# Layer 2's projections: 192 channels contracted as 128 + 64 rows instead of 96 + 96

## The chip, the cores and the metric

The kernel runs on one core of one Trainium2 chip. The metric is the device time of one execution in microseconds (us); what is quoted is the median over runs. Everything in the kernel is fp32. The engines of the core work side by side: TensorE (PE; its weight loads are listed apart as PEld), VectorE (DVE), ScalarE (ACT), GpSimd (POOL), and SyncE (SP), which here issues nearly all DMAs. A DMA is carried out by some or all of 16 DMA engines.

## The reference

Four layers are applied to an image batch x of shape (4, 64, 64, 192), each as `x = x + layer(groupnorm(x))`. Layers 0, 1 and 3 are selective scans (state-space models) over rows and columns. The change touches only layer 2, a gated Toeplitz mixer with D1 = 576 inner channels:

```python
p = silu(x @ p_w.T + p_b)            # x: normalized input, 192 channels -> 576
q = silu(x @ q_w.T + q_b)
v = silu(x @ v_w.T + v_b)
# a1, a2: 128 Toeplitz coefficients per channel, from a small MLP and a decay
qv = q * v
o1 = toeplitz(qv along w, a1)
o2 = toeplitz(qv along h, a2)
out = (p * (o1 + o2)) @ o_w.T + o_b
```

The three projections p, q and v contract 192 channels. They are the matmuls that the change rearranges; `o_w` contracts 576 channels and stays as it is.

## The kernel before, in words

Names: B = 4 images, L = 4096 pixels each, C = 192 channels kept in DRAM as KC = 2 halves of PC = 96 (partition, half, pixel), chunks of T = 512 pixels, NCH = 8 chunks per image, D1 = 576 inner channels as KD = 6 tiles of PD = 96. All of layer 2 is in `toeplitz`, and it runs after layer 1's scans and before layer 3's. It has three parts.

**Normalization.** Per image, layer 1's parts are added to the input, the sum goes to DRAM as `t_x` and its group norm as `t_xn`.

**The q/v part** (pool `t_*`). For each inner tile t (6) the two Toeplitz matrices `mat` are loaded (four DMAs, L931); for each group g of two images (2), so in twelve passes, it does:

- 16 chunks. Each loads `xn`, 96 x 2 x 512 (L60, the helper `load`), computes q and v (L944: two matmuls each, one for every half of the channels, accumulated in one PSUM tile each), applies Silu on ACT (L948) and multiplies into `qv` on DVE (L951).
- two calls of `toeplitz_way`: PE transposes (L1006), 64x64 matmuls with the matrices (L1014), transposes back (L1019), with evacuations on DVE and ACT.
- two stores of the result to DRAM, `t_o` (L956).

The pool `t_s` has two buffers per name, so the load of chunk i+2 can be issued only when PE has finished reading chunk i. The PSUM pool has four one-bank buffers under one tag.

**The p part** (pool `p_*`), for 32 chunks: load `xn`, `xr` (the residual) and `o` (`t_o`); six tiles of p (L975, two matmuls each), Silu (L978), multiply by `o` on DVE (L979), project back with `o_w` (L984: 2 x 6 matmuls), add the residual on DVE (L987), store (L990).

An fp32 matmul appears in the trace as two LDWEIGHTS/MATMUL pairs, called passes here; so a 192-channel product of one 96-channel tile over 512 pixels is 2 matmuls and 4 passes.

Instructions are written in program order and put into each engine's queue by the Tile framework, which may move independent work ahead; an engine then runs its queue in order. SP runs its queue in order too: a DMA that waits for a buffer holds back the DMAs behind it.

Two other places are used for comparison. `fetch` (L312) loads a scan operand twice, once into each half of the partitions, with one DMA:

```python
one = pools[name].tile([128, T], F32, name=name)
src = job["deltas" if name == "both" else "dtus"][key * 64 : (key + 1) * 64, :]
nc.sync.dma_start(one, src.unsqueeze(0).broadcast_to([2, 64, T]))
```

`step_size` (L253) multiplies 12 rows at partitions 32 to 43 and 12 rows at 96 to 107, into two PSUM tiles of 128 channels and 256 pixels.

Of the kernel before, what the change touches and what calls it, by code (L numbers as in the profile page):

```python
# [7 lines left out]
F32 = mybir.dt.float32  # L8
AF = mybir.ActivationFunctionType
# [4 lines left out]
B, HW, L = 4, 64, 4096  # L14
C = 192
PC, KC = 96, 2
# [3 lines left out]
T = 512  # L20
# [16 lines left out]
class Kernel:  # L37
# [807 lines left out]
    def toeplitz(self, x_in, parts, x_out):  # L845

        tc, nc, ins = self.tc, self.nc, self.i
        pre = "L2_"
        xn_d, x_d = self.image_tiles("t_xn"), self.image_tiles("t_x")
        o_d = [self.dram.tile([PD, KD, L], F32, name=f"t_o{b}") for b in range(B)]  # L850
        coef = [self.dram.tile([D1, 128], F32, name=f"t_a{j}") for j in range(2)]
        M = 127
        with (
            tc.tile_pool(name="n", bufs=2) as pn,
            tc.tile_pool(name="n_w", bufs=1) as pw,
            tc.tile_pool(name="n_ps", bufs=2, space=PSUM) as psum,
        ):
            fb = self.load(pw, "fb", ins["L1_fc_b"])
            for b in range(B):
                x = pn.tile([PC, KC, L], F32, name="x")  # L860
                rows, cols = (pn.tile([PC, KC, L], F32, name="part") for _ in range(2))
                for k in range(KC):
                    for to, of in ((x, x_in[b]), (rows, parts[b][0]), (cols, parts[b][1])):
                        nc.sync.dma_start(to[:, k, :], of[:, k, :])
                for k in range(KC):
                    nc.vector.scalar_tensor_tensor(
                        x[:, k, :], x[:, k, :], fb[:, k : k + 1], rows[:, k, :], ALU.add, ALU.add
                    )
                    by_row = x[:, k, :].rearrange("p (a b) -> p a b", b=HW)
                    nc.vector.tensor_add(by_row, by_row, cols[:, k, :].rearrange("p (b a) -> p a b", b=HW))  # L870
                    nc.sync.dma_start(x_d[b][:, k, :], x[:, k, :])
                self.group_norm(x, pn, psum)
                nc.sync.dma_start(xn_d[b], x)

            pos = self.load(pw, "pos", ins["c_pos"])
            power = pw.tile([PD, 128], F32, name="power")
            nc.sync.dma_start(power, ins["c_power"].broadcast_to([PD, 128]))
            rate = self.load(pw, "rate", ins[f"{pre}slope"])
            nc.vector.tensor_scalar(rate, rate, 0.0, 1.0, ALU.max, ALU.min)
            nc.vector.tensor_scalar(rate, rate, 1.0 - 0.95, 0.95, ALU.mult, ALU.add)  # L880
            nc.scalar.activation(rate, rate, AF.Ln)
            decay = pw.tile([PD, KD, 128], F32, name="decay")
            for t in range(KD):
                nc.scalar.activation(decay[:, t, :], power, AF.Exp, scale=rate[:, t : t + 1])
            for j in range(2):
                q = f"{pre}t{j + 1}_"
                w0 = self.load(pw, "w0", ins[q + "w0"])
                b0 = self.load(pw, "b0", ins[q + "b0"])
                ws = self.load(pw, "ws", ins[q + "ws"])
                bs = self.load(pw, "bs", ins[q + "bs"])  # L890
                wo = self.load(pw, "wo", ins[q + "wo"])
                bo = self.load(pw, "bo", ins[q + "bo"])
                ps = psum.tile([32, 128], F32, name="mlp_ps")
                nc.tensor.matmul(ps, w0, pos, start=True, stop=True)
                h = pn.tile([32, 128], F32, name="mlp_h")
                nc.scalar.activation(h, ps, AF.Relu, bias=b0)
                for i in range(3):
                    ps = psum.tile([32, 128], F32, name="mlp_ps")
                    nc.tensor.matmul(ps, ws[:, i, :], h, start=True, stop=True)
                    h = pn.tile([32, 128], F32, name="mlp_h")  # L900
                    nc.scalar.activation(h, ps, AF.Relu, bias=bs[:, i : i + 1])
                for t in range(KD):
                    ps = psum.tile([PD, 128], F32, name="a_ps")
                    nc.tensor.matmul(ps, wo[:, t * PD : (t + 1) * PD], h, start=True, stop=True)
                    a = pn.tile([PD, 128], F32, name="a")
                    nc.vector.scalar_tensor_tensor(
                        a, ps, bo[:, t : t + 1], decay[:, t, :], ALU.add, ALU.mult
                    )
                    nc.sync.dma_start(coef[j][t * PD : (t + 1) * PD, :], a)
# [4 lines left out]
        with (  # L914
            tc.tile_pool(name="t_w", bufs=1) as pw,
            tc.tile_pool(name="t_big", bufs=1) as big,
            tc.tile_pool(name="t_s", bufs=2) as sp,
            tc.tile_pool(name="t_ps", bufs=4, space=PSUM) as psum,
        ):
            wq, wv = (self.load(pw, n, ins[f"{pre}{n}"]) for n in ("q_w", "v_w"))  # L920
            bq, bv = (self.load(pw, n, ins[f"{pre}{n}"]) for n in ("q_b", "v_b"))
            for t in range(KD):
                ch = slice(t * PD, (t + 1) * PD)

                mats = []
                for j in range(2):
                    m = big.tile([128, PD, HW], F32, name=f"mat{j}")
                    a = coef[j][ch, :]
                    src = bass.AP(a.tensor, a.offset, [[1, HW], [128, PD], [1, HW]])
                    for half in range(2):  # L930
                        nc.sync.dma_start(m[half * HW : (half + 1) * HW], src)  # L931
                    mats.append(m)
                for g in range(B // G):

                    qv = big.tile([PD, G, L], F32, name="qv")
                    for b in range(G):
                        for c in range(NCH):
                            s = slice(c * T, (c + 1) * T)
                            xn = self.load(sp, "xn", xn_d[g * G + b][:, :, s])
                            two = []  # L940
                            for wt, bias, name in ((wq, bq, "q"), (wv, bv, "v")):
                                ps = psum.tile([PD, T], F32, name=f"{name}_ps", tag="ps")
                                for k in range(KC):
                                    nc.tensor.matmul(  # L944
                                        ps, wt[:, k, ch], xn[:, k, :], start=k == 0, stop=k == KC - 1
                                    )
                                r = sp.tile([PD, T], F32, name=name)
                                nc.scalar.activation(r, ps, AF.Silu, bias=bias[:, t : t + 1])  # L948
                                two.append(r)
                            turned = qv[:, b, L - (c + 1) * T : L - c * T][:, ::-1]  # L950
                            nc.vector.tensor_mul(turned, two[0], two[1])  # L951
                    o = big.tile([PD, G, L], F32, name="o")
                    for j in range(2):
                        self.toeplitz_way(j, qv, o, mats[j], big, psum, NI)
                    for b in range(G):
                        nc.sync.dma_start(o_d[g * G + b][:, t, :], o[:, b, :])  # L956

        with (
# [1 line left out]
            tc.tile_pool(name="p_s", bufs=2) as sp,  # L960
            tc.tile_pool(name="p_ps", bufs=4, space=PSUM) as psum,
        ):
            wp, bp = self.load(pw, "wp", ins[f"{pre}p_w"]), self.load(pw, "bp", ins[f"{pre}p_b"])
            wo, bo = self.load(pw, "wo", ins[f"{pre}o_w"]), self.load(pw, "bo", ins[f"{pre}o_b"])
            for b in range(B):
                for c in range(NCH):
                    s = slice(c * T, (c + 1) * T)
                    xn = self.load(sp, "xn", xn_d[b][:, :, s])
                    xr = self.load(sp, "xr", x_d[b][:, :, s])
                    o = self.load(sp, "o", o_d[b][:, :, s])  # L970
                    p = sp.tile([PD, KD, T], F32, name="p")
                    for t in range(KD):
                        ps = psum.tile([PD, T], F32, name="p_ps")
                        for k in range(KC):
                            nc.tensor.matmul(  # L975
                                ps, wp[:, k, t * PD : (t + 1) * PD], xn[:, k, :], start=k == 0, stop=k == KC - 1
                            )
                        nc.scalar.activation(p[:, t, :], ps, AF.Silu, bias=bp[:, t : t + 1])  # L978
                    nc.vector.tensor_mul(p, p, o)  # L979
                    xo = sp.tile([PC, KC, T], F32, name="xo")  # L980
                    for m in range(KC):
# [6 lines left out]
                            xo[:, m, :], ps, bo[:, m : m + 1], xr[:, m, :], ALU.add, ALU.add  # L988
                        )
                    nc.sync.dma_start(x_out[b][:, :, s], xo)  # L990

    def toeplitz_way(self, j, qv, o, mat, big, psum, NI):

# [159 lines left out]
```

## Time and profile before

| | us |
|---|---|
| median of 3 runs | 31505.68 (31467.85 to 31518.7) |
| the profiled execution | 31496.9 |
| its span | 31495.0 |
| busy: PE | 28016.1 (89%) |
| busy: PEld | 13777.8 (44%) |
| busy: DVE | 22496.5 (71%) |
| busy: ACT | 23230.4 (74%) |
| busy: POOL | 22921.2 (73%) |

The span is the time from the first to the last instruction of one profiled execution. A group line gives the source line, engine, operation, tiles (output <- inputs), shapes and count, then busy time and mean duration of one, then the idle time just before them with what ended it. A MATMUL's duration includes the pipeline's latency; what counts for throughput is the distance between starts.

Layer 2 lies between about 22,030 us and 25,110 us of the span, 3.1 ms of 31.5. The rest of the span belongs to the scans of layers 0, 1 and 3.

### The profile page before, as it was taken

The numbers are of one execution on the slowest core, as the hardware profiler recorded it, in microseconds if no ns is written. First come the engines' busy times: TensorE is split into PE (matmuls) and PEld (weight loads), VectorE is DVE, ScalarE is ACT, GpSimd is POOL, SyncE is SP. The second block draws the span as 40 slices with busy tenths as digits, with TensorE's granted clock in tenths as the row PEclk, the third lists the DMA queues.
The fourth block names the chain that finished last, engine by engine and source line by source line (L and its number), as shares of the span: only waits on it lengthen the run. The fifth ranks groups of instructions, "written<-read, shape, count | busy, mean of one in ns | idle before, by whom it ended". The sixth has DMA issues, their size and how long they took to land.

```text
span 31495.0 us, 452842 instructions
## 1 busy us (share of the span) xinstructions
PE 28016.1 (89%) x164120; PEld 13777.8 (44%) x164120; DVE 22496.5 (71%) x16587; ACT 23230.4 (74%) x50559; POOL 22921.2 (73%) x9863
## 2 busy tenths in 40 slices
PE   8998998998899699999999999999588988888888
PEld 4554554554455344444444444444355343434344
DVE  7887887888788677777777777777433267677767
ACT  7885885887688488888888888888123187878788
POOL 7885885887688488888888888888000086867777
PEclk9999998999999899999999999999789999999999
DMA  3333333334333433233332333333533454444444
GB/s 105 101 100 114 103 99 115 100 98 112 102 102 100 134 94 93 93 98 98 98 99 92 94 94 96 98 99 98 133 73 71 109 133 121 129 126 127 124 127 125
DMA packets 1586996, 3327.52 MB, mean 106 GB/s; under 512 B 354981, under 2 KB 374166, under 8 KB 1569142
## 3 DMA queue, kind: packets, MB, share of 16 engines
q1 hardware_dynamic: 1418870, 3021.63, 35.1%
q10 hardware_dynamic: 165888, 276.91, 2.6%
q8 instruction: 1299, 21.28, 0.3%
q14 instruction: 939, 7.69, 0.1%
HBM read 2138.38 MB, written 656.08 MB: 89 GB/s over the span
## 4 chain that ended last, share of the span: by engine, by line
PE 39%; DVE 14%; POOL 14%; ACT 13%; DMA 10%; issue 7%; SPq 2%; ACTq 0%; DVEq 0%; POOLq 0%
PE b L360 16%; POOL hc L405 11%; DVE h L400 8%; PE y L423 8%; ACT diag L318 5%; ACT dA L383 4%; DVE h L393 3%; DMA xn<-m_col 3%; DMA xn<-m_row 2%; PE in_ps L777 2%; POOL bs L337 2%; SPq L325 2%; PE yt_ps L1014 2%; PE conv_ps L509 2%; DMA xn<-t_xn 2%
## 5 line engine op out<-in xcount | busy, mean ns | idle before, releaser
L405 POOL TENSOR_TENSOR hc<-h,c 128x1024 f32<-128x1024 f32 x7680 | 18176.9, 2384 | 3019.2 <-DVE h L393 1288.0
L360 PE MATMUL b<-diag,dtuT 128*64 128x256 f32 x98304 | 12662.5, 392 | 955.3 <-DVE h L400 829.9
L360 PEld LDWEIGHTS b<-diag,dtuT 128*64 128x64 f32 x98304 | 7451.4, 140 | 6835.4 <-issue 3023.8
L400 DVE TENSOR_TENSOR_SCAN h<-dA,carry,b 128x512 f32<-128x512 f32 x6720 | 8187.4, 1264 | 1696.7 <-PE b L360 875.4
L423 PE MATMUL y<-hc,fold 128*64 128x512 f32 x30720 | 8832.2, 601 | 579.8 <-POOL hc L405 566.2
L383 ACT ACTIVATE dA<-both,A 128x512 f32<-128x512 f32 (+1 forms) x12288 | 8306.5, 711 | 305.7 <-DVE h L393 181.0
L393 DVE TENSOR_TENSOR_SCAN h<-dA,b 128x1024 f32<-128x1024 f32 x2304 | 5251.9, 2284 | 2064.3 <-PE b L360 900.9
L318 ACT ACTIVATE diag<-ident,bt 128x128 f32<-128x128 f32 x20480 | 6514.8, 391 | 123.5 <-ACT b L383 83.2
L337 POOL TENSOR_TENSOR bs<-dtu,bc 128x1024 f32<-128x1024 f32 x1536 | 3639.0, 2369 | 300.0 <-DMA dtu<-dtu 172.2
L423 PEld LDWEIGHTS y<-hc,fold 128*64 128x64 f32 x30720 | 2462.3, 138 | 2969.2 <-POOL hc L405 1263.2
L477 POOL MEMSET pad<- 128x13068 f32 (+1 forms) x8 | 73.5, 9187 | 3972.7 <-DMA cw<-in_L_conv_w 3005.2
L383 ACT ACTIVATE b<-both,A 128x504 f32<-128x504 f32 (+1 forms) x3072 | 2077.4, 676 | 283.0 <-DVE h L400 237.0
L393 DVE TENSOR_TENSOR_SCAN h<-b,bs 128x1024 f32<-128x1024 f32 x768 | 1754.3, 2284 | 658.6 <-ACT b L383 387.6
L403 ACT COPY carry<-h 128x2 f32<-128x2 f32 x4608 | 849.6, 184 | 1233.8 <-DVE h L400 1015.3
L400 DVE TENSOR_TENSOR_SCAN h<-b,carry,bs 128x512 f32<-128x512 f32 x1344 | 1638.2, 1259 | 105.5 <-POOL hc L405 94.2
L400 DVE TENSOR_TENSOR_SCAN h<-dA,b 128x512 f32<-128x512 f32 x960 | 1112.4, 1205 | 425.3 <-ACT dA L383 165.4
L383 ACT ACT_TABLE_LOAD x1018 | 1306.1, 1283 | 16.8 <-ACT b L371 0.3
L777 PE MATMUL in_ps<-xn,in_w 96*128 96x512 f32 x1536 | 943.6, 746 | 333.4 <-DMA xn<-m_row 173.3
L794 DVE SCALAR_TENSOR_TENSOR u<-in_ps,conv_w,u 128x504 f32<-128x504 f32 (+2 forms) x1152 | 835.8, 725 | 475.3 <-ACT u L789 454.0
L269 DVE TENSOR_TENSOR dtu<-delta,u 128x1536 f32<-128x1536 f32 (+1 forms) x256 | 607.4, 2373 | 541.6 <-ACT delta L268 541.6
L278 PEld LDWEIGHTS dtu_ps<-ident,dtu 128*128 128x128 f32 (+1 forms) x4096 | 421.5, 142 | 874.2 <-issue 554.0
L777 PE MATMUL z_ps<-xn,in_w 96*128 96x512 f32 x1536 | 761.7, 618 | 0.3 <-ACT dtuT L281 0.2
(163 smaller groups left out, 21940.7 us busy)
## 6 DMA issues: line engine op xcount, KB each, us to landing
c<-bc_dram SPq DMA_DIRECT2D x3072, 256.0 KB
both<-delta SPq DMA_DIRECT2D x2048, 128.0 KB
bc<-bc_dram SPq DMA_DIRECT2D x768, 256.0 KB
both<-delta_dram SPq DMA_DIRECT2D x768, 256.0 KB
dtu<-dtu_dram SPq DMA_DIRECT2D x768, 256.0 KB
dtu<-dtu SPq DMA_DIRECT2D x1280, 128.0 KB
L_y<-out ACTq DMA_DIRECT2D x512, 256.0 KB
u<-L_u SPq DMA_DIRECT2D x160, 768.0 KB
```

Of the source, the lines that this page charges most:

```text
L318: nc.scalar.activation(to, self.ident, AF.Copy, scale=of)
L325: nc.sync.dma_start(one[q * 64 : (q + 1) * 64, :], src.unsqueeze(0).broadcast_to([64, 2 * T]))
L337: self.nc.gpsimd.tensor_mul(by(b), dtu, by(job["bbc"][p]))
L360: nc.tensor.matmul(to, job["dtuT"][:, k, g * 64 : (g + 1) * 64], job["diag"][p][:, k, 2 * q : 2 * q + 2, :], start=True, stop=True,)
L383: nc.scalar.activation(to[n], of, AF.Exp, scale=w["A"][:, g, 2 * p + n : 2 * p + n + 1])
L393: nc.vector.tensor_tensor_scan(h[:, way], dA[:, way], b[:, way], 0.0, ALU.mult, ALU.add)
L400: nc.vector.tensor_tensor_scan(hn[:, n, way], dA[:, n, way], by_n[:, n, way], start, ALU.mult, ALU.add)
L403: nc.scalar.copy(carry[g, p], hn[:, :, 0 if rev else T - 1])
L405: nc.gpsimd.tensor_mul(hc, h, job["cbc"][p])
L423: nc.tensor.matmul(y[c * 64 : (c + 1) * 64, :], self.fold, of, start=first == 0 and n == 0, stop=last == LAST and n == 1)
L777: nc.tensor.matmul(ps, w["in_w"][:, k, to + t * P : to + (t + 1) * P], job["xn"][:, k, :], start=k == 0, stop=k == KC - 1,)
L794: nc.vector.scalar_tensor_tensor(u[:, :, to], ps[:, :, of], tap(3 - j), u[:, :, to], ALU.mult, ALU.add)
```

## The change

`t_xn` is stored in DRAM as 192 plain rows. The weights of q, v and p are cut into a piece of the first 128 channels and a piece of the last 64; the second piece is held twice, in partitions 0 to 63 and in 64 to 127 (`load_apart`). The pixels of a chunk come as two tiles of 128 partitions: the first 128 channels, and the last 64 twice (`load_pixels`, two DMAs). Two results at a time are computed (`project_two`): q and v of a chunk, or two neighbouring tiles of p. Each gets one matmul over 128 rows; then each gets one over 64 rows, the first result from partitions 0 to 63 and the second from 64 to 127.

```diff
-        xn_d, x_d = self.image_tiles("t_xn"), self.image_tiles("t_x")
+        xn_d = [self.dram.tile([C, L], F32, name=f"t_xn{b}") for b in range(B)]
+        x_d = self.image_tiles("t_x")
...
-                nc.sync.dma_start(xn_d[b], x)
+                nc.sync.dma_start(xn_d[b].rearrange("(k p) l -> p k l", p=PC), x)
...
-            wq, wv = (self.load(pw, n, ins[f"{pre}{n}"]) for n in ("q_w", "v_w"))
+            wq, wv = (self.load_apart(pw, n, ins[f"{pre}{n}"]) for n in ("q_w", "v_w"))
...
-                            xn = self.load(sp, "xn", xn_d[g * G + b][:, :, s])
-                            two = []
-                            for wt, bias, name in ((wq, bq, "q"), (wv, bv, "v")):
-                                ps = psum.tile([PD, T], F32, name=f"{name}_ps", tag="ps")
-                                for k in range(KC):
-                                    nc.tensor.matmul(
-                                        ps, wt[:, k, ch], xn[:, k, :], start=k == 0, stop=k == KC - 1
-                                    )
-                                r = sp.tile([PD, T], F32, name=name)
+                            xn = self.load_pixels(sp, xn_d[g * G + b][:, s])
+                            pair = [psum.tile([PD, T], F32, name=f"{name}_ps", tag="ps") for name in "qv"]
+                            self.project_two(pair, [[one[:, ch] for one in wt] for wt in (wq, wv)], xn)
+                            two = [sp.tile([PD, T], F32, name=name) for name in "qv"]
+                            for r, ps, bias in zip(two, pair, (bq, bv)):
                                 nc.scalar.activation(r, ps, AF.Silu, bias=bias[:, t : t + 1])
-                                two.append(r)
...
-            wp, bp = self.load(pw, "wp", ins[f"{pre}p_w"]), self.load(pw, "bp", ins[f"{pre}p_b"])
+            wp, bp = self.load_apart(pw, "wp", ins[f"{pre}p_w"]), self.load(pw, "bp", ins[f"{pre}p_b"])
...
-                    xn = self.load(sp, "xn", xn_d[b][:, :, s])
+                    xn = self.load_pixels(sp, xn_d[b][:, s])
...
-                    for t in range(KD):
-                        ps = psum.tile([PD, T], F32, name="p_ps")
-                        for k in range(KC):
-                            nc.tensor.matmul(
-                                ps, wp[:, k, t * PD : (t + 1) * PD], xn[:, k, :], start=k == 0, stop=k == KC - 1
-                            )
-                        nc.scalar.activation(p[:, t, :], ps, AF.Silu, bias=bp[:, t : t + 1])
+                    for t in range(0, KD, 2):
+                        pair = [psum.tile([PD, T], F32, name="p_ps") for _ in range(2)]
+                        ws = [[one[:, (t + j) * PD : (t + j + 1) * PD] for one in wp] for j in range(2)]
+                        self.project_two(pair, ws, xn)
+                        for j, ps in enumerate(pair):
+                            nc.scalar.activation(p[:, t + j, :], ps, AF.Silu, bias=bp[:, t + j : t + j + 1])
...
+    def load_apart(self, pool, name, w):
+
+        nc, cut = self.nc, 128 - PC
+        a, b = (pool.tile([128, w.shape[2]], F32, name=f"{name}{j}") for j in range(2))
+        nc.sync.dma_start(a[0:PC], w[:, 0, :])
+        nc.sync.dma_start(a[PC:128], w[0:cut, 1, :])
+        for h in range(2):
+            nc.sync.dma_start(b[h * 64 : (h + 1) * 64], w[cut:PC, 1, :])
+        return a, b
+
+    def load_pixels(self, pool, x):
+
+        n = x.shape[1]
+        a, b = (pool.tile([128, n], F32, name=f"xn{j}") for j in range(2))
+        self.nc.sync.dma_start(a, x[0:128, :])
+        self.nc.sync.dma_start(b, x[128:C, :].unsqueeze(0).broadcast_to([2, C - 128, n]))
+        return a, b
+
+    def project_two(self, pair, ws, x):
+        for ps, w in zip(pair, ws):
+            self.nc.tensor.matmul(ps, w[0], x[0], start=True, stop=False)
+        for h, (ps, w) in enumerate(zip(pair, ws)):
+            rows = slice(h * 64, (h + 1) * 64)
+            self.nc.tensor.matmul(ps, w[1][rows], x[1][rows], start=False, stop=True)
```

## The prediction

> **What bounds the kernel now.** First the grouped instructions of the stretch that holds layer 2 (22,030 to 25,110 us), the rows of the projections:
>
> ```profile
> L944 PE MATMUL q_ps<-xn,q_w 96*96 96x512 f32 x768 | 405.3, 654 | 238.3 <-DMA xn<-t_xn 227.6 <-DMA q_w<-in_L_q_w 7.0 <-ACT v L948 1.7
> L944 PE MATMUL v_ps<-xn,v_w 96*96 96x512 f32 x768 | 380.1, 619 | 0.0
> L984 PE MATMUL o_ps<-p,wo 96*96 96x512 f32 x768 | 339.9, 599 | 4.2 <-DVE p L979 4.2
> L975 PE MATMUL p_ps<-xn,wp 96*96 96x512 f32 x768 | 338.1, 597 | 21.2 <-DMA xn<-t_xn 21.2
> ```
>
> There are 192 q/v chunks and 32 p chunks. The last column tells the two parts apart: PE stood idle 227.6 us before q for the load of `xn`, but only 21.2 us before p, all at the first chunk. Next, PE's timeline and the length of the p part by windows:
>
> ```profile
> 22461.80 1.88 PE L944 MATMUL q_ps<-xn,q_w 96*96 96x512 f32 x4
> 22463.52 1.88 PE L944 MATMUL v_ps<-xn,v_w 96*96 96x512 f32 x4
> 22465.90 1.93 PE L944 MATMUL q_ps<-xn,q_w 96*96 96x512 f32 x4 [0.50 <-DMA xn<-t_xn]
> 22467.66 1.88 PE L944 MATMUL v_ps<-xn,v_w 96*96 96x512 f32 x4
> 22469.38 1.88 PE L944 MATMUL q_ps<-xn,q_w 96*96 96x512 f32 x4
> 24434.00:25090.00 656.00, 655.77 (x1512) 244.84 (x1512) 150.31 (x93) 130.49 (x191) 0.00 (x0) 0.99 0.43 114
> ```
>
> Passes start 0.429 us apart, so a q/v chunk costs PE 8 x 0.429 = 3.43 us. But chunk starts alternate: 4.10 (61.80 to 65.90), then 3.48. The load for the chunk at 65.90 was issued by SP at 22461.99, when the chunk two before it had freed its buffer: 3.9 us from issue to use, longer than one chunk. With two buffers, two chunks take 4.10 + 3.43 = 7.53 us. So the q/v part is bound by **the load's latency plus one chunk's PE time**. The p part is bound by PE alone (655.77 busy of 656), 20.6 us a chunk.
>
> In each of the twelve q/v passes the first two chunks are preloaded. The third waits behind stores of `o` or loads of `mat`, some 13 to 22 us. From the third chunk's start to the end of the 16th the timeline gives 54.9 to 56.3 us, mean 55.5.
>
> **The doubled load.** The new b tile is filled by one DMA whose source is a broadcast of 64 rows of 2 KB over two halves. L312 has just that form. A 3 us stretch in which one such load moves alone, and one with an ordinary `xn` load, by windows (last two columns: busy share of the 16 DMA engines, GB/s), then the packets of the first stretch:
>
> ```profile
> 10888.00:10891.00 3.00, 3.00 (x21) 1.50 (x21) 2.39 (x2) 2.95 (x5) 2.42 (x3) 1.00 0.13 51
> 22463.00:22465.20 2.20, 2.20 (x6) 0.65 (x4) 0.46 (x1) 0.68 (x1) 0.00 (x0) 1.00 0.58 177
> ```
>
> ```profile
> DMA packets 74, 0.15 MB, mean 51 GB/s; under 512 B 0, under 2 KB 0, under 8 KB 74
> ```
>
> 0.13 of 16 engines is two engines: 74 packets in 3 us on two is 81 ns each. The load issued at 10884.51 ended at about 10891.8.
>
> [...] a start that follows a pass of another tiling comes at 522 ns instead of 429. [...]
>
> ```profile
> 357.90 0.70 PE L253 MATMUL dt_ps<-xd,dtw 12*128 12x256 f32 x4
> ```
>
> Its four passes start as two pairs, 6 to 7 ns apart within a pair. [...] Here windows of 3.41 us with PE streaming under 0.3 of the time were nearly all followed by half clock, and it took about 0.9 to come back.
>
> **The change part by part.**
>
> *PE.* A pair goes from 8 passes to 4 full and 4 half-row passes that run two by two: 6 slots, 2.57 us. Each pair changes tiling twice. [...] the second pass's weight load is no longer hidden: 78 ns for 96 columns (starts 506 apart after such a change at L821). Twice 171 is 0.345. A pair costs 2.92 us instead of 3.43.
>
> *p part.* Three pairs save 3 x 0.51 = 1.53 us per chunk, 32 x 1.53 = **-49 us**. Loads: engines 0 and 1 (I assume the doubled load keeps to the same two) get 64 packets of b, 8 of a, 12 each of `xr` and the store, 36 of `o`, 132 x 105 ns (median here) = 14 us in 19: hidden, since `xn` is asked for a whole chunk ahead. DVE's multiply (3.36 us) is covered by the next chunk's first p passes before L984 begins. As both results of a pair now end together, ACT needs 0.68 us more before it; uncovered, that would be 22 us. I take 0.
>
> *q/v part.* Per chunk, a is 128 packets over 16 engines, 8 each, and b 128 packets over two, 64 each. Those two engines take 64 x 0.081 + 8 x 0.108 (mean packet with all 16 busy) = 6.05 us per chunk. PE needs 2.92 and ACT 2 x 0.68, so **two DMA engines become the bound**. PE then streams under half of the time and its clock should drop at times. A chunk at half clock takes some 5.5 us, which delays the buffer and thus the next issue: a period of 6.6 to 6.9. I take 6.3 on the mean. From third start to end: 13 x 6.3 + 3.7 (landing to start 0.8, last chunk 2.92) + 1.5 for a last chunk that may be slow = 87.1 against 55.5, +31.6. The third chunk starts later by 60 packets on those engines, 4.9, less the 0.5 by which chunk 0 ends sooner: +4.4. So 36.0 x 12 = **+432 us**. Transposes that begin at a low clock: 1.5 x 12 = +18.
>
> *SP.* One more issue per chunk, 224 x 0.54 us: SP has the time, as a's issue can go when the full passes end, before b's buffer is free. What queues behind a b that waits is the next chunk's a, and at a pass's end the stores of `o`; both wait for later work anyway. Weights: nine more DMAs of about 0.43 us, at most +4. The store of `t_xn` has the same runs of 16 KB: 0. SBUF tiles and PSUM banks: a pair holds two of four banks, so one chunk can be evacuated while the next fills; 0, as ACT's 1.37 us fits in any period above.
>
> Sum: 432 + 18 - 49 + 4 = +405. On 31496.9 that is 31,902; the median shown is 9 above the profiled run, so I say **31,905 us**.
>
> Bounds of the unknowns. Low: the two engines at 81 ns throughout (5.85 a chunk), no clock loss: 12 x (13 x 5.85 + 3.7 - 55.5 + 4.4) - 49 = +295. High: 97 ns a packet (mean duration in that L312 load, 7.07 a chunk), clock loss, nothing gained in p: 12 x 47.5 = +570.
>
> **Rivals.**
>
> 1. *The doubled load spreads over all engines* (faster). Its rows lie 16 KB apart in DRAM, where L312's are contiguous, so the pattern could be laid out differently. Then 16 packets per engine and chunk; a is asked for before b, and b has 8 packets where `xn` had 12, so latency falls from 4.1 to about 3.8. Two chunks take 3.8 + 2.92 = 6.72 instead of 7.53: 0.40 x 14 x 12 = -68, with p -117: 31,380. It decides as soon as b has four engines or more (16 packets a chunk or 32: 1.3 to 2.6 us, under PE's 2.92). Against it: 2 is the first dimension in both.
> 2. *The half-row passes don't run together* (the change doesn't do what it says). Then a pair has 8 slots and two tiling changes, 3.78. In q/v the two engines mostly hide that (+3 us a pass, +40); p turns from -49 to 96 x 0.345 = +33: about 32,025. L253 speaks against it. With rival 1 also true, q/v stays near 7.6 per two chunks and the total near 31,540.
>
> **How the numbers follow.** The two-engine case 0.86, with its lesser form (rival 2) 0.04 more; rival 1 0.07; both rivals 0.03. A change under 0.2% (63 us) can't be told from none by a measurement of this kernel. Range: 31,760 to 32,080 takes in the bounds; what it leaves out is rival 1 and about a tenth of the main case. Faster 0.07, same 0.03, slower 0.90.
>
> **What would show it.** Right: in the stretch of a q/v pass, the DMA share falls towards 0.15 to 0.2, PE's idle before q_ps goes to some 3 us a chunk ended by the second `xn` tile, chunk starts 5.9 to 7 us apart, half-clock windows inside the pass; in p, 19.1 us a chunk and half-row passes in pairs some 7 ns apart. Wrong: chunk starts under 4 us apart (rival 1), or single half-row passes 0.43 us apart (rival 2).

## The result and the profile after

| | before | after |
|---|---|---|
| median, us | 31512.19 (31467.85 to 31524.38, 4 runs) | 31820.6 (31780.63 to 31829.44, 4 runs) |
| span of the profiled execution | 31495.0 | 31778.8 |
| start to the first q matmul | 22411.7 | 22379.9 |
| q/v part (first q to first p matmul) | 2022.5 | 2348.7 |
| p part (start of the first p matmul to start of the last residual add) | 673.1 | 661.5 |
| from there to the end | 6387.6 | 6388.7 |

The ratio of the times is 1.0099, 95% interval 1.0087 to 1.0111: slower by 308 us. The two parts that were changed give 326.2 - 11.6 = +315. The first row differs by -32 between these two profiles, though most of what lies in it are scans that were not touched: over all profiles of this study, the kernel before with its variants included, it lies anywhere between 22,380 and 22,475. So parts are compared here part by part, and whole kernels by their medians.

The rows of the projections after, grouped as before:

```profile
L1009 PE MATMUL q_ps<-xn,q_w 128*96 128x512 f32 x384 | 279.9, 820 | 153.9 <-DMA xn<-t_xn 143.2 <-DMA q_w<-in_L_q_w 6.1 <-DVE o L1049 4.3
L1012 PE MATMUL q_ps<-xn,q_w 64*96 64x512 f32 x384 | 262.9, 771 | 397.2 <-DMA xn<-t_xn 396.4
L1012 PE MATMUL v_ps<-xn,v_w 64*96 64x512 f32 x384 | 262.9, 771 | 0.0
L979 PE MATMUL o_ps<-p,wo 96*96 96x512 f32 x768 | 341.2, 601 | 28.2 <-DVE p L974 28.2
L1012 PE MATMUL p_ps<-xn,wp 64*96 64x512 f32 x384 | 106.7, 633 | 7.1 <-DMA xn<-t_xn 7.1
```

PE's idle time for pixels was 227.6 us. Now 396.4 us lie ahead of the half-row passes alone, which read the doubled tile b, and 143.2 ahead of the full ones. By the trace, the wait at the third chunk of each pass is a large part of both sums: 195.1 us before and 224.3 after. What is new lies in the chunks behind it: some 35 us of waiting before, some 316 after. PE's timeline in a q/v pass, then SP's issues of b in the same stretch:

```profile
22437.01 1.13 PE L1012 MATMUL q_ps<-xn,q_w 64*96 64x512 f32 x1 [3.00 <-DMA xn<-t_xn]
22437.01 1.14 PE L1012 MATMUL v_ps<-xn,v_w 64*96 64x512 f32 x1
22437.94 1.06 PE L1012 MATMUL q_ps<-xn,q_w 64*96 64x512 f32 x1
22437.95 1.06 PE L1012 MATMUL v_ps<-xn,v_w 64*96 64x512 f32 x1
22438.94 1.85 PE L1009 MATMUL q_ps<-xn,q_w 128*96 128x512 f32 x2
22440.62 1.02 PE L1009 MATMUL v_ps<-xn,v_w 128*96 128x512 f32 x2
22442.87 0.67 PE L1012 MATMUL q_ps<-xn,q_w 64*96 64x512 f32 x1 [1.23 <-DMA xn<-t_xn]
```

```profile
22439.06 0.49 SPq L1004 DMA_DIRECT2D xn<-t_xn  x1
22444.04 0.50 SPq L1004 DMA_DIRECT2D xn<-t_xn  x1
```

The half-row passes of q and v start together: they do run side by side. The full passes of the next chunk (22438.94) go ahead as soon as a is there, and then PE stands before the half-row passes until b lands; those come at 37.01 and 42.87. SP asks for a new b as soon as the half-row passes have let go of its buffer (22439.06), while the other buffer's b is still on its way. Over all twelve passes, from the fourth chunk on, half-row passes are 5.96 us apart (3.82 us from chunk to chunk before). The DMA view of a stretch of such chunks (22,445 to 22,508 us), in 40 slices (busy share of the 16 engines in tenths, then GB/s):

```profile
DMA  1511151111333311133151111232411133151111
GB/s 51 192 51 49 52 191 48 52 49 51 124 117 118 126 49 51 51 130 116 49 186 57 51 51 49 98 143 87 157 52 49 49 109 134 51 187 56 62 49 51
```

The slices of about 50 GB/s are b alone, at the rate of the doubled L312 load: from 22,449.8 to 22,452.8 us the DMA share is 0.13 at 51 GB/s, as there, which is two engines' worth of 16. The peaks come where a is loaded as well (0.76 and 230 GB/s from 22,442.8 to 22,444.0 us).

In the p part, one chunk's change to the output projection:

```profile
25011.51 3.35 DVE L974 TENSOR_TENSOR p<-p,o 96x3072 f32<-96x3072 f32 x1 [5.35 <-ACT p L973]
25012.01 1.10 PE L1012 MATMUL p_ps<-xn,wp 64*96 64x512 f32 x4
25013.04 1.10 PE L1009 MATMUL p_ps<-xn,wp 128*96 128x512 f32 x2
25014.92 1.53 PE L979 MATMUL o_ps<-p,wo 96*96 96x512 f32 x3 [0.78 <-DVE p L974]
```

From half rows to full rows the starts lie 25013.04 - 25012.01 = 1.03 us apart, which is 2 slots of 0.429 and 0.17 for the change of tiling. Then PE waits for the DVE multiply, 28.2 us over the 32 chunks (the row of L979). Chunks in p are 20.08 us apart; they were 20.71.

### The profile page after: what moved, and what is told of

It is laid out like the page before. It is cut to its first block, busy times and chain, and to the rows that moved or that the text cites. A ratio compares the mean times of both kernels' runs of the same rounds, so it can differ in the third digit from the quotient of the medians.

```text
span 31778.8 us, 453302 instructions
## 1 busy us (share of the span) xinstructions
PE 27945.1 (88%) x164120; PEld 13657.4 (43%) x164120; DVE 22503.7 (71%) x16587; ACT 23194.3 (73%) x50559; POOL 22908.5 (72%) x9863
## 5 line engine op out<-in xcount | busy, mean ns | idle before, releaser
L945 ACT ACTIVATE q<-q_ps,q_b 96x512 f32<-96x512 f32 x192 | 131.0, 682 | 1238.6 <-PE v_ps L1012 1238.6
L947 DVE TENSOR_TENSOR qv<-q,v 96x512 f32<-96x512 f32 x192 | 132.1, 688 | 1085.0 <-ACT v L945 1085.0
```

## The experiments

The theory: the doubled load runs on two DMA engines and sets the pace of the q/v part; PE is not the bound there. The rival: PE's tiling changes and low clock, or the bytes moved. In p: the gain of 1.53 us a chunk is there, but PE waits 0.9 us of it for the multiply. Each line of the table is one kernel. The reference for e1 to e4 was the kernel before on their chip, 31523.95 us; for e5 to e8 it was 31519.33. The parts are cut as in the first table, from the profile.

| | median us | ratio to before, 95% | q/v | p |
|---|---|---|---|---|
| e1 b by two DMAs | 31347.26 | 0.9929 to 0.9954 | 1871.9 | 650.9 |
| e2 half rows in turn | 31909.1 | 1.0110 to 1.0138 | 2382.3 | 708.7 |
| e3 before + doubled DMA | 32148.74 | 1.0185 to 1.0213 | 2613.8 | 673.2 |
| e4 multiply in two | 31816.49 | 1.0081 to 1.0109 | 2347.0 | 644.7 |
| e5 two DMAs, multiply in three | 31314.99 | 0.9927 to 0.9955 | 1875.8 | 612.4 |
| e6 one DMA from 256 rows | 31451.11 | 0.9972 to 0.9985 | 1952.5 | 652.0 |
| e7 before, four buffers | 31376.61 | 0.9949 to 0.9974 | 1880.7 | 672.5 |
| e8 as e5, four buffers | 31225.34 | 0.9899 to 0.9927 | 1798.8 | 612.7 |

### e1: b by two DMAs

```diff
-        self.nc.sync.dma_start(b, x[128:C, :].unsqueeze(0).broadcast_to([2, C - 128, n]))
+        for h in range(2):
+            self.nc.sync.dma_start(b[h * 64 : (h + 1) * 64], x[128:C, :])
```

> The changed kernel, with the tile b of the pixels filled by two DMAs of 64 rows each instead of one that broadcasts the rows over [2, 64, 512]. Bytes, tiles and matmuls stay. Theory (the one doubled DMA keeps to two engines and sets the q/v part's pace): [...] chunk starts fall from 5.96 us to about 3.0 us, near PE's 2.92, since only b waits for the end of a chunk and its flight is covered by the next full passes. The q/v part loses some 2.9 x 14 x 12 = 490 us: about 31,330 us in all (31,280 to 31,420). Rival (the pace comes from PE's tiling changes and low clock, or from the bytes moved): no change or slower by the extra issue, 31,800 to 31,850.

Measured: 31347.26 us, 473 below the changed kernel. PE's timeline:

```profile
23690.09 0.67 PE L1013 MATMUL q_ps<-xn,q_w 64*96 64x512 f32 x1
23691.12 1.10 PE L1010 MATMUL q_ps<-xn,q_w 128*96 128x512 f32 x2
23692.06 1.02 PE L1010 MATMUL v_ps<-xn,v_w 128*96 128x512 f32 x2
23693.01 0.67 PE L1013 MATMUL q_ps<-xn,q_w 64*96 64x512 f32 x1
```

The same stretch by windows (length, then busy time of PE, PEld, DVE, ACT and POOL, clock, DMA share, GB/s):

```profile
23673.00:23710.00 37.00, 37.00 (x101) 10.38 (x100) 8.25 (x12) 16.35 (x26) 0.00 (x0) 0.99 0.59 177
```

Half-row passes every 2.92 us, PE busy for all 37 us, at 177 GB/s instead of 86 over the stretch of the DMA view above. The bytes, tiles and matmuls are those of the changed kernel, and there is one more issue per chunk: how b was loaded is what cost the 473 us. The trace doesn't list the engines of each DMA; that b now has many more than two is read from the rate and from the DMA share of 0.59, where b alone had 0.13. Why the two forms differ isn't shown.

### e2: the half rows in turn

```diff
-        for h, (ps, w) in enumerate(zip(pair, ws)):
-            rows = slice(h * 64, (h + 1) * 64)
+        for ps, w in zip(pair, ws):
+            rows = slice(0, 64)
```

> The changed kernel, with both half-row matmuls of a pair taken from partitions 0 to 63, so that they run one after the other. Loads stay. Theory: in the q/v part two DMA engines are the bound and PE has 3 us to spare per chunk, so the two more slots (0.86 us a chunk) mostly vanish there, +0 to +40 us over all; in the p part, which PE bounds, three pairs cost 3 x 0.86 = 2.6 us more per chunk, less up to 0.9 us of idle time before the output projection: +53 to +82. Together 31,870 to 31,940 us. Rival (PE bounds q/v as well, by its low clock): 288 pairs x 0.86 = +247 or more, 32,070 us or above.

Measured: 31909.1. The q/v part took 33.6 us longer than with pairs, where 192 x 0.86 = 165 us of PE time were added:

```profile
22502.43 1.10 PE L1012 MATMUL q_ps<-xn,q_w 64*96 64x512 f32 x2 [1.08 <-DMA xn<-t_xn]
22503.37 1.02 PE L1012 MATMUL v_ps<-xn,v_w 64*96 64x512 f32 x2
22504.31 1.10 PE L1009 MATMUL q_ps<-xn,q_w 128*96 128x512 f32 x2
22505.25 1.02 PE L1009 MATMUL v_ps<-xn,v_w 128*96 128x512 f32 x2
22508.61 1.10 PE L1012 MATMUL q_ps<-xn,q_w 64*96 64x512 f32 x2 [2.34 <-DMA xn<-t_xn]
```

Now q's two passes come before v's, and PE still waits for b. In p the distance grew by 1.54 to 21.62 us, +47.2 us in all, a little under the expected range. Of the 2.57 us added to each chunk, the wait for the multiply took up 0.75 (L979 now waits 4.2 us in the whole part, as before the change, and not 28.2); the other 0.3 stays open. So row pairing is real, and here it was worth time only in p, where PE is the bound.

### e3: the kernel before, plus a doubled DMA that nothing reads

```diff
                             xn = self.load(sp, "xn", xn_d[g * G + b][:, :, s])
+                            self.load(sp, "xnb", xn_d[g * G + b][0:64, 1, s].unsqueeze(0).broadcast_to([2, 64, T]))
```

(`load` gives this tile the shape 128 x T.)

> The kernel before, with its own loads and matmuls, and one more DMA per q/v chunk of the form in question: 64 rows of 2 KB broadcast over [2, 64, 512] into a tile of its own that nothing reads. [...] Theory: engines 0 and 1 get 64 packets of it and 12 of the chunk's own load, 64 x 0.081 + 12 x 0.096 = 6.3 us a chunk, so the ordinary load is late behind them: chunk starts go from 4.0 to about 6.3 us, 12 x 13 x 2.3 = +360 us, 31,870 us (31,800 to 31,950), as slow as the changed kernel without any of its matmuls. Rival (256 KB more per chunk over 16 engines, about 1.3 us at most in the way): 31,510 to 31,650 us.

Measured: 32148.74, some 280 above the expectation. As nothing reads the tile, nothing held the extra DMA to one per chunk: SP's queue has two of them for each chunk, and more between the passes, until all 192 were issued, the last at the start of the fourth of the twelve passes. SP's timeline at the last of them, and a stretch while they ran by windows:

```profile
23563.14 21.30 SPq L60 DMA_DIRECT2D xnb<-t_xn  x5
```

```profile
23300.00:23560.00 260.00, 161.21 (x1136) 99.07 (x1136) 49.58 (x58) 46.87 (x72) 0.00 (x0) 0.73 0.20 69
```

Five issues, each 5.2 us after the one before, as it waits for a buffer that the one two before it fills. While they ran, chunk starts were 12.5 us apart (from the third chunk of a pass on); after the last, in the same run, 3.97, as in the kernel before (4.00). The arithmetic of the expectation with two such DMAs, 128 x 0.081 + 12 x 0.096, gives 11.5, so it was short by 1 us a chunk. The size was missed, and the expectation left out that SP's queue is in order: an ordinary load was issued 5 to 6 us after the start of the last pass that read its buffer (0.6 in the kernel before), as it stood behind an extra DMA that waited. Then it took 12.3 us from issue to use, where it was 3.96. The two delays weren't told apart by a run, so the size can't be carried over to one doubled DMA per chunk. But on and off in one run shows the point: 192 of these DMAs, with none of the change's matmuls, make the q/v part slower by more than the change did (591 us against 326).

### e4: the multiply in two

```diff
-                    nc.vector.tensor_mul(p, p, o)
+                    for part in (slice(0, 4), slice(4, 6)):
+                        nc.vector.tensor_mul(p[:, part, :], p[:, part, :], o[:, part, :])
```

> The changed kernel, with the p part's DVE multiply of 6 tiles by o cut into one over the first 4 tiles and one over the last 2. Theory (the p part gained 0.63 us a chunk instead of 1.53 because both results of the last pair end together, so ACT's second 0.68 us and the 3.36 us multiply are no longer covered by the next chunk's passes, 0.93 us idle before the output projection): only 2 tiles, about 1.15 us, are left to do after the last pair; chunk distance in p falls from 20.08 to about 19.15 us, 31 x 0.93 = -29 us, some 31,790 us, at the edge of what the times can tell but plain in the profile. Rival (the gain is missing because tiling changes cost more than 0.345 us a pair): the distance stays at 20.08.

Measured: 31816.49, which can't be told from the changed kernel, and 19.88 us between chunks: neither the 19.15 of the theory nor the rival's 20.08. L980 still waits 23.8 us in all. The timeline shows why:

```profile
25106.67 1.10 PE L1013 MATMUL p_ps<-xn,wp 64*96 64x512 f32 x4
25108.52 10.54 PE L980 MATMUL o_ps<-p,wo 96*96 96x512 f32 x24 [0.74 <-DVE p L975]
```

The Tile framework now puts the output projection straight behind the last pair, with no pass of the next chunk between, and PE waits for the first multiply (2.29 us over four tiles, which can start only when the second pair is evacuated). The wait moved; the theory was not decided by this run.

### e5: two DMAs, the multiply in three

e1, and the slices of e4 as (0, 2), (2, 4), (4, 6).

> The changed kernel with b filled by two DMAs of 64 rows, and the p part's multiply cut into three of two tiles each, one per pair. Theory (the p part's missing gain is PE waiting for the multiply, and with a cut at four tiles PE still waits 0.82 us for the first, 2.29 us long multiply): each multiply of 1.2 us starts when its own pair is evacuated, and 8 passes of the output projection lie ahead of the last one's use; distance in p from 20.08 to 10.38 + 3 x 2.92 = 19.14 us, 31 x 0.94 = -29 us against the version with two DMAs alone (31,347): 31,318 us (31,290 to 31,350). Rival (tiling changes or the order of PE's queue cost the rest): 19.9 or more a chunk, no difference.

Measured: 31314.99, 32 below e1, at the edge of what the times can tell; the profile is plain. Distance in p 19.06 us, p part 612.4, and the output projection waits for nothing:

```profile
L980 PE MATMUL o_ps<-p,wo 96*96 96x512 f32 x768 | 337.3, 595 | 0.0
```

So the gain that each chunk of p lacked was the wait for DVE. With it gone a chunk costs 20.71 - 19.06 = 1.65 us less than before, against 1.53 in the prediction's sum.

### e6: one DMA for both pixel tiles

```diff
-        xn_d = [self.dram.tile([C, L], F32, name=f"t_xn{b}") for b in range(B)]
+        xn_d = [self.dram.tile([256, L], F32, name=f"t_xn{b}") for b in range(B)]
...
+                nc.sync.dma_start(xn_d[b][C:256, :], x[128 - PC : PC, 1, :])
...
-        a, b = (pool.tile([128, n], F32, name=f"xn{j}") for j in range(2))
...
+        t = pool.tile([128, 2, x.shape[1]], F32, name="xn")
+        self.nc.sync.dma_start(t, x.rearrange("(k p) l -> p k l", p=128))
```

> The changed kernel, with the last 64 channels stored a second time in DRAM (256 rows, one more store of 1 MB per image) and each chunk's two pixel tiles loaded by one DMA of 128 x 2 x 512 over all 16 engines. Theory (two DMAs were as fast as 2.92 us a chunk because a is asked for when the full passes end, a third of a chunk earlier than b): with one tile the whole load waits for the end of the chunk and the full passes wait for all of it; two chunks take some 4.1 to 4.5 us of load plus 2.92, so 3.5 to 3.7 us a chunk, +0.7 x 13 x 12 = +110 us against two DMAs (31,347): 31,455 us (31,400 to 31,520), still faster than the kernel before. Rival (only the number of engines matters): 2.9 to 3.0 a chunk and 31,330 to 31,360.

Measured: 31451.11 (21 runs), 104 above e1, of which 80.6 lie in q/v; where the rest lies isn't shown. Chunk starts alternate 2.9 and 3.9 to 4.0 us. From the fourth chunk on, half-row passes are 3.46 us apart on the mean, where e1 has 2.94, so the loss is three quarters of the 0.7 us expected:

```profile
24137.39 0.59 PE L1011 MATMUL q_ps<-xn,q_w 64*96 64x512 f32 x1
24138.01 1.07 PE L1008 MATMUL q_ps<-xn,q_w 128*96 128x512 f32 x2
24141.93 1.07 PE L1008 MATMUL q_ps<-xn,q_w 128*96 128x512 f32 x2 [0.96 <-DMA xn<-t_xn]
```

This is the pattern of the kernel before: load latency plus one chunk. The DMA share is 0.50 at 146 GB/s from 24,130 to 24,150 us, so here too the loads are far from two engines' 0.13, and yet the chunks are slower than e1's. So the number of engines isn't all: e1 has two tiles that are asked for and released at different times. It also has three smaller DMAs for the one here, and no run tells these two apart.

### e7 and e8: four buffers

e7 is the kernel before with `bufs=4` for `xn` in the q/v part; e8 is e5 with `bufs=4` for the pixel tiles.

> The kernel before, with four buffers instead of two for the pixels xn in the q/v part. Theory (before, the q/v part was bound by load latency plus PE, not by PE): a chunk falls from 4.00 to PE's 3.43 to 3.5 us, 13 x 0.5 x 12 = -80 us, and two more preloaded chunks shorten the wait near the start of each pass by 2 x 3.45, 6.9 x 12 = -83: about 31,350 us (31,310 to 31,430), as fast as the changed matmuls with two DMAs and two buffers. Rival (PE bound): 31,500 to 31,530.

> The changed kernel with b filled by two DMAs, the multiply in three, and four buffers for the pixel tiles everywhere. Theory: chunks already stand at PE's 2.92 us, so only the wait near the start of each q/v pass gets shorter, by two more preloaded chunks, 2 x 2.92 x 12 = -70 us against the same with two buffers: about 31,250 us (31,200 to 31,300). Against the kernel before with four buffers the 6-slot pairs would then be worth 16 x 0.51 x 12 = 98 us in q/v, less what the wait for stores and matrices takes back, and up to 49 in p.

Measured: 31376.61 and 31225.34. In e7 PE waits for pixels only ahead of the fifth chunk of a pass, and runs the others without a gap:

```profile
23690.44 1.88 PE L944 MATMUL q_ps<-xn,q_w 96*96 96x512 f32 x4
23692.16 1.88 PE L944 MATMUL v_ps<-xn,v_w 96*96 96x512 f32 x4
23693.88 1.88 PE L944 MATMUL q_ps<-xn,q_w 96*96 96x512 f32 x4
```

Two more buffers bring the kernel before 142.7 us, with its matmuls untouched. Some 60 us of it are the pace (3.43 us a chunk where it was 3.82, 13 chunks in 12 passes). Another 62 are the wait at the start of each pass, 195.1 us in all ahead of the third chunk and now 132.6 ahead of the fifth; the last 20 or so stay open. So before the change PE wasn't the bound of q/v. With the pace of the loads out of the way in both (the wait at the start of the passes stays, 138.9 us in e8), the paired form with the multiply in three is worth 151 us (e8 against e7): 81.9 in q/v and 59.8 in p by the profiles. e8 is the fastest kernel here, 294 us under the one before.

## Why the prediction was right

It gave +405 us, with a range of +263 to +583 over the profiled run; +308 was measured. The mechanism held; the sizes of several terms did not. For q/v the sum had 450 us where 326 were measured, for p -49 where it was -11.6. The two errors have opposite signs, and that they cancel in part is luck.

- **Two DMA engines become the bound.** Held: e1 takes the bound away, e3 puts it into the kernel before (with a delay in SP's queue on top), e2 shows PE idle beside it. That L312's two engines would carry over to b, whose rows lie 16 KB apart, was an estimate from one load; b alone then showed the same share of 0.13, at 49 to 52 GB/s in its slices. Rival 1's premise was wrong. Its price too: with b no longer on two engines (e1) the gain over the kernel before was 177 us and not 117. The q/v part fell by 151 where the price had 68, since only b waits for the end of a chunk; a's load is asked for earlier and its full passes cover b's flight. The p part fell by 22 where the price had 49.
- **6.05 us per chunk from the packets.** Measured 5.96.
- **6.3 on the mean, for PE's low clock.** Too much. The clock did fall: by the trace's clock record 572 of the 1292 us of the twelve chunk stretches were at half clock, against 269 of 972 before. But the period stayed at 5.96: from the fourth chunk on, the 64 periods that were mostly at half clock took 5.85 us on the mean, the 80 others 6.05 (in the timeline above, half-row passes 0.93 us apart at half clock, and the next b in use 5.86 later). The step that failed: it let all six slots of a chunk follow b's landing before the next b could be asked for. Only the two half-row slots do, as SP's issue at 22439.06 shows, and the other buffer's b is on its way meanwhile. Two engines stayed busy, and a slow PE hid behind them. Over 13 periods that is 4.4 us a pass.
- **3.7 + 1.5 for the last chunk.** For the same reason it is 1.0 to 2.0 us, mean 1.4, from b's first use in the last chunk to the first transpose behind it; 3.8 us a pass too much.
- **The third chunk later by 4.4.** Counted from the start of a pass, its half-row passes start 2.6 us later than the third chunk before (second group of a tile, g = 1) or 3.7 (g = 0, apart from the first pass with 7.1); 3.4 on the mean, 1.0 too much.
- So a pass, from its first q matmul to its first transpose, grew from 80.8 to 107.6 us, **+26.8 instead of +36.0**, and the stretch from there to the next pass by 0.4 instead of 1.5: q/v +326 where the sum had 450.
- **p: -49.** Measured -11.6. The slot arithmetic held: 6 slots and 0.345 us per pair are the 2.92 us between pairs in the timelines (e1), and e5 gained all of it. The 0.171 for one change of tiling was 522 - 429 = 93 ns at the first start behind it and 78 at the second; in the p part after, nearly all first starts come 519 to 523 ns after the last pass of the other tiling, and the second ones 506 or 507 ns after the first. What PE does in this time isn't shown. What failed is "I take 0" for the multiply: the cover was gone, and PE waited 28.2 us in all (the uncovered price given was 22). And at the start of p, b on two engines put off the first result by 7.3 us, a term that the sum didn't have: the first residual add comes 30.6 us after the first p matmul instead of 23.3. PE waits 4.5 us for the first chunk's b and 2.5 for the second's, whose passes stand ahead of the first output projection; these are the 7.1 us in the row of L1012. In e1 the add comes after 21.0 us, and in e4, where the projection goes ahead of the second chunk, after 23.5.
- **Rival 2** fell with the timeline after: q's and v's half-row passes start within 0.01 us of each other.

## What to carry to other kernels

When a load is rewritten, look before anything else at the DMA share and the rate while it moves alone: a broadcast over two halves in one DMA moved 256 KB in 5.2 us here, at a share of 0.13, and two plain DMAs of the same bytes took 473 us off the kernel. Before making PE shorter, see from the distance of chunk starts (3.82 us in the kernel before, where PE needed 3.43) whether PE is what sets the pace; here two more buffers gave the old matmuls about half of what all changes together gave. And when results are made to end together, count what the evacuating engines still have to do after them.

## What the runs showed that was not expected

- Two tiles that become free at different times, 256 KB each, gave 2.94 us a chunk, and one tile of 512 KB gave 3.46 with the same bytes and matmuls (e1 and e6), with two buffers in both.
- PE at half clock cost nothing measurable while two DMA engines were the bound (period 5.96 us, with 572 of the 1292 us of the chunk stretches at half clock).
- One DMA of the doubled form that nobody waits for slowed the chunks from 3.97 to 12.5 us when two of them ran per chunk (e3). An ordinary load then took 12.3 us from issue to use instead of 3.96, though the DMA share was only 0.20.
